# Seven products for eight inside one block product of each large product, with the sums taken in PSUM, and a re-planned order of work

## The chip, the cores and the metric

The kernel runs on one core of one Trainium2 chip. The metric is the device time of one execution in microseconds (us). The core's TensorE (PE) multiplies matrices into PSUM, VectorE (DVE) and ScalarE (ACT) read PSUM and work on tiles in SBUF, GpSimd (POOL) works on SBUF alone, and SyncE (SP) is used here only to issue DMAs. Each engine runs its own instructions in the order in which they stand, and waits on semaphores for the others.

## The reference

Inputs are x, 128 graphs of 128 nodes with 512 features, one adjacency matrix, and the weights of four layers; everything is fp32. Each layer adds a graph operation to x and normalises over the features:

```
x = layernorm(x + norm_adj @ (x @ W0) + bias)                      # layer 0
x = layernorm(x + L1(x, adj, adj, b))                              # layer 1
x = layernorm(x + (rel / norm(rel)) @ (x @ Wv.T))                  # layer 2
       where rel = adj.T * ((x @ Wq.T) @ (x @ Wk.T).T)
x = layernorm(x + elu(att @ h + beta * h))                         # layer 3
       where h = x @ W3, att = softmax(leaky_relu(s1 + s2.T) * adj)
       and s1, s2 are h times the two halves of a vector a
...
L1: A = W1 @ x;  C = W2 @ x + b;  out[o, i] = max over j of relu(A[o, j] + (C - A)[o, i])
```

In layer 1 both weights are the same adjacency, so C - A is the bias b alone, and out is the same for all features i of a row; the normalisation over the features takes such a constant away. So the kernel makes nothing for this layer but its normalisation, which it folds into that of layer 0. Layer 2's two weights Wq and Wk are folded into one matrix gq before the first group. So each group of graphs needs four large products with a 512x512 weight: w (layer 0), z and v (layer 2) and k (layer 3).

## The kernel before

Work goes in 32 groups (NG) of GB = 4 graphs, so the left side of a large product is 512x512 as well (4 graphs of 128 rows by 512 features). The seven products of `Product` split both sides into 2x2 blocks of 256x256 and make seven block products for eight, with sums and differences of blocks taken beforehand:

- `w_sum` (line 371) makes four differences of weight blocks once; they lie in a tile of four blocks, called `w_t`, `gq_t` or `wvT_t`.
- `Left.sum` makes four sums of left blocks for every group, on POOL (`pool_tt`, line 422), each 128x512; the tile is `S_y`, `S_x` or `S_n`. w has its own left side y; z and v share the sums of the transposed x; k has those of n, a later x transposed.
- `Product.make(i)` (line 540) makes block product i by four matmuls of 128x256 (two row halves, two chunks of the contraction) into one PSUM bank. `ONTO` lets products 6, 3 and 4 accumulate onto the banks of 1, 5 and 7. The order is 1, 2, 5, 7, 6, 3, 4.
- `first`, `add`, `take`, `last` carry the banks into the result: ACT copies (line 416), DVE additions of a bank and a block (line 419), and one POOL addition. For w the result is added straight into x by `d_onto` and `u_onto`.

Around the four products a group has: the aggregation with the adjacency (py, line 702), three normalisations (bn_stats and bn_aggr on DVE, a power of -0.5 on POOL in `inv_sqrt`, line 425, and the application on ACT, line 762), `pe_r` for rel (line 817), `left_times` for rel @ v and att @ h (line 866), the attention's softmax (`sc`, `pl`, `ej`, `ei`, `exp`, `rd`, `so`), and two transposes of x: `square` on DVE turns 32x32 blocks, and sixteen DMAs on SP (line 487) move them into place.

Nothing schedules this at run time. The order of every engine's work is written out by hand as strings of steps: `2.z6` is product 6 of z of group 2 counted from a base. In a name the prefixes c, d, t, u are first, add, take, last; cy, sy are the copy and the sums of y; xt, xd the turn and the move of x; nt, nd those of n; st, va, po, nb, ap the normalisation; bi the bias of layer 0. `HEAD` holds the setup (`s.`) and the first groups, `TURN` is one period of the loop and is repeated for each group in the middle, and `TAIL` holds the last groups:

```python
FIRST = 6
LAST = -10
...
for base, steps in (
    [(0, HEAD)] + [(g - BACK, TURN) for g in range(FIRST, end)] + [(end - BACK, TAIL)]
):
    for group, name in (t.split(".") for t in steps.split()):
        todo[group if group == "s" else base + int(group)].step(name)
```

PSUM gives six rotating banks of 128x512 fp32 to these steps, two more hold the vector for the attention scores (`wa_bc`). x has five buffers, the transposed left sides have three. In the setup, DVE forms that vector by eight multiplications with a sum (`q`, line 638), and PE spreads it over the partitions by eight transposes (`wa`, line 653); PE is warmed by `WARM` = 7 transposes. In the last group, k is made plainly (`k_plain`, line 792): four matmuls of 128x512 for each graph, then the copy, att @ h, elu, normalisation and the output, graph by graph.

Of the kernel before, what the change touches and what calls it, by code (L numbers as in the profile page):

```python
# [45 lines left out]
WARM = 7  # L46
GB = 4
# [15 lines left out]
1.w5 1.dw2 1.sy2 1.w7 1.dw5 0.pow 1.sy3 1.w6 1.dw7 0.nbw 2.sy2 0.apw0 1.w3 0.apw1 0.xt0 1.bi10
0.apw2 0.xt1 1.w4 0.apw3 1.dw3 2.sy3 0.xt2 1.tw 1.bi00 0.xt3 2.w1 1.dw4 0.xd 1.bi11 2.w2 2.dw1
1.bi01 2.w5 2.dw2 1.uw10 1.uw01 2.w7 2.dw5 1.uw11 1.stw0 2.w6 2.dw7 2.bi10 1.stw1 2.w3 2.tw
1.stw2 2.bi00 1.stw3 2.bi11 2.w4 2.dw3 1.vaw 2.bi01 3.y10 2.dw4 1.pow 3.y00 3.cy10 0.sx0 3.y11
3.cy00 3.y01 3.cy11 1.nbw 0.sx1 1.apw0 0.z1 1.apw1 1.xt0 0.sx2 1.apw2 1.xt1 0.z2 2.uw01 0.cz1
1.xt2 1.apw3 0.sx3 2.stw0 0.z5 3.cy01 0.dz2 2.uw10 1.xt3 0.z7 0.cz5 2.stw1 1.xd 2.uw11 0.z6
0.dz7 3.sy0 2.stw2 3.sy1 2.stw3 0.z3 0.tz 2.vaw 0.uz11 0.z4 0.dz3 2.pow 3.sy2 0.r0 0.dz4 0.r1
2.nbw 3.sy3 2.apw0 0.r2 2.apw1 3.bi10 0.r3 2.apw2 0.v1 0.rm 2.apw3 3.bi00 0.rt 0.sq0 0.sq1  # L70
3.bi11 0.wr 0.v2 0.cv1 0.sq2 3.bi01 2.xt0 0.sq3 0.v5 0.dv2 1.sx0 2.xt1 0.cr 2.xt2 0.v7 0.cv5
1.sx1 2.xt3 1.sx2 0.v6 0.dv7 0.rp 0.v3 0.tv 1.sx3 0.uv11 0.v4 0.dv3 1.z1 2.xd 0.dv4 1.z2 1.cz1
1.z5 1.dz2 1.z7 1.cz5 1.z6 1.dz7 1.z3 1.tz 1.uz11 1.z4 1.dz3 0.f0 1.dz4 2.sx0 0.f1 0.fa0 0.f2
0.stv0 2.sx1 0.f3 0.fa1 0.fa2 2.sx2 1.r0 0.fa3 1.r1 2.sx3 0.stv1 1.r2 0.stv2 1.r3 0.stv3 2.z1
1.rm 0.vav 1.sq0 1.rt 0.pov 1.sq1 2.z2 1.wr 2.cz1 0.nbv 1.sq2 0.apv0 2.z5 2.dz2 0.apv1 0.nt0
0.apv2 0.sc00 1.cr 2.z7 2.cz5 0.nt1 0.apv3 0.nt2 2.z6 1.sq3 2.dz7 1.rp 0.nt3 0.sc01 2.z3 2.tz
0.sc10 2.uz11 0.sc11 2.z4 2.dz3 0.sc20 2.r0 2.dz4 0.sc21 2.r1 0.sc30 2.r2 0.sc31 2.r3 0.pw 1.v1
2.rm 2.rt 2.sq0 2.sq1 2.wr 1.v2 1.cv1 2.sq2 2.sq3 1.v5 2.rp 1.dv2 0.pe 1.v7 1.cv5 1.v6 1.dv7
0.pl0 0.pl1 1.v3 1.tv 0.pl2 1.uv11 0.pl3 1.v4 1.dv3 0.ej 0.ei 1.f0 1.dv4 0.ex0 1.f1 0.ex1 1.fa0
0.ex2 1.f2 1.fa1 0.ex3 1.f3 1.stv0 3.w1 2.cr 0.rd 1.fa2 0.so0 0.so1 0.so2 3.w2 3.dw1 0.so3 1.fa3  # L80
3.w5 3.dw2 0.at 3.w7 1.stv1 0.aw 3.dw5 1.stv2 3.w6 3.dw7 1.stv3 0.cat 3.w3 3.tw 1.vav 3.uw01
3.w4 3.uw10 3.dw3 3.stw0 3.uw11 4.y10 0.nd 3.dw4 4.y00 3.stw1 4.cy10 1.pov 3.stw2 4.y11 4.cy00
4.bi10 3.stw3 4.y01 4.cy11 4.sy1 3.vaw 4.w1 4.cy01 1.nbv 4.sy0 1.apv0 4.w2 4.dw1 1.apv1 1.sc00
3.pow 1.apv2 1.sc01 4.w5 4.sy2 1.apv3 3.nbw 1.sc10 4.sy3 3.apw0 4.w7 4.dw5 3.apw1 4.bi00 1.sc11
3.apw2 4.w6 4.dw7 3.apw3 4.bi01 1.sc20 4.w3 4.tw 1.sc21 4.bi11 3.xt0 0.sn0 1.sc30 4.w4 3.xt1
0.sn1 3.xt2 2.v1 3.xt3 0.sn2 1.sc31 2.v2 4.dw2 2.cv1 1.pw 4.uw01 4.dw4 0.sn3 4.dw3 2.v5 2.dv2
4.uw10 4.stw0 2.v7 2.cv5 4.stw1 1.pe 4.uw11 2.v6 2.dv7 4.stw2 4.stw3 2.v3 2.tv 1.pl0 2.uv11
4.vaw 1.pl1 1.pl2 2.v4 2.dv3 1.pl3 4.pow 1.ej 2.f0 3.xd 2.dv4 2.f1 1.ei 2.fa0 2.f2 1.ex0 1.ex1
2.fa1 2.f3 1.ex2 2.fa2 0.k1 1.ex3 2.fa3 1.rd 2.stv0 0.k2 0.ck1 1.so0 1.so1 1.so2 1.so3 0.k5
0.dk2 1.at 2.stv1 0.k7 0.ck5 2.stv2 1.aw 2.stv3 0.k6 0.dk7 2.vav 4.nbw 0.k3 2.pov 0.tk 4.apw0  # L90
1.nt0 0.uk11 4.apw1 1.nt1 0.k4 0.dk3 4.apw2 3.sx0 1.nt2 4.apw3 0.h0 0.dk4 3.sx1 1.nt3 0.h1 3.sx2
0.em0 1.nd 0.h2 0.em1 0.ee0 0.h3 3.sx3 0.em2 0.ee1 3.z1 0.em3 0.ee2 0.ea0 0.ee3 0.ea1 3.z2 3.cz1
0.ea2 0.ea3 3.z5 3.dz2 0.stk0 0.stk1 3.z7 3.cz5 0.stk2 0.stk3 3.z6 3.dz7 1.cat 0.vak 2.nbv 3.z3
3.tz 0.pok 2.apv0 3.uz11 2.apv1 3.z4 3.dz3 2.apv2 1.sn0 2.apv3 3.r0 3.dz4 1.sn1 3.r1 0.nbk 2.nt0
1.sn2 3.r2 0.apk0 2.sc00 0.apk1 3.r3 0.fin0 1.sn3 2.nt1 0.apk2 0.fin1 1.k1 3.rm 0.apk3 0.fin2
2.nt2 3.sq0 0.fin3 1.k2 3.rt 1.ck1 2.nt3 3.sq1 3.wr 3.sq2 2.sc01 2.nd 1.k5 3.sq3 1.dk2 3.rp
2.sc10 1.k7 1.ck5 2.sc11 2.sc20 2.sc21 1.k6 1.dk7 2.sc30 1.k3 1.tk 2.sc31 1.uk11 1.k4 1.dk3 1.h0
1.dk4 1.h1 1.em0 5.ld 3.cr 1.h2 1.ee0 1.em1 1.ea0 1.h3 1.ee1 1.em2 3.v1 1.em3 1.ee2 2.sn0 2.pw
1.ea1 1.ee3 3.v2 1.ea2 2.sn1 3.cv1 1.ea3 2.sn2 1.stk0 3.v5 3.dv2 2.sn3 2.pe 1.stk1 3.v7 3.cv5
1.stk2 1.stk3 3.v6 3.dv7 2.pl0 1.vak 4.xt0 2.pl1 1.pok 3.v3 2.pl2 4.xt1 3.tv 1.nbk 2.pl3 4.xt2  # L100
3.uv11 1.apk0 3.v4 3.dv3 1.apk1 1.fin0 4.xt3 1.apk2 1.fin1 2.ej 5.y10 1.apk3 4.xd 3.dv4 5.y00
5.bi10 5.cy10 2.ei 5.y11 5.cy00 5.bi00 2.ex0 5.y01 5.cy11 5.sy1 3.f0 5.cy01 2.ex1 3.f1 3.fa0
5.sy0 2.ex2 3.f2 3.stv0 2.ex3 5.bi11 3.f3 3.fa1 3.fa2 5.w1 5.sy2 3.fa3 3.stv1 5.bi01 5.w2 5.dw1
5.sy3 3.stv2 1.fin2 5.w5 3.stv3 1.fin3 2.rd 3.vav 2.so0 5.w7 5.dw5 3.pov 2.so1 3.nbv 5.w6 2.so2
3.apv0 6.ld 5.dw7 4.sx0 3.apv1 3.nt0 4.sx1 3.apv2 5.w3 3.nt1 3.apv3 3.nt2 4.sx2 5.tw 3.nt3 5.w4
2.so3 5.dw2 4.sx3 2.k1 2.at 5.uw01 5.dw4 2.aw 3.sc00 2.k2 2.ck1 5.uw10 5.dw3 3.sc01 5.uw11 2.k5
5.stw0 2.cat 5.stw1 2.k7 2.ck5 5.stw2 5.stw3 2.k6 2.dk7 5.vaw 2.dk2 5.pow 3.sc10 2.k3 2.tk 5.nbw
3.sc11 2.uk11 5.apw0 2.k4 3.sc20 5.apw1 2.dk3 5.apw2 3.sc21 5.apw3 6.y10 3.nd 2.dk4 6.y00 6.cy10
6.bi10 3.sc30 6.y11 6.cy00 3.sc31 6.bi00 6.y01 6.cy11 6.sy0 4.z1 6.cy01 6.sy1 4.z2 4.cz1 6.sy2
4.z5 4.dz2 6.bi11 6.sy3 4.z7 4.cz5 6.bi01 3.pw 4.z6 4.dz7 4.z3 4.tz 5.xt0 3.sn0 5.xt1 3.pe 4.z4  # L110
# [179 lines left out]
def kernel(  # L290
# [124 lines left out]
    def copy(o, i):  # L415
        nc.scalar.copy(o, i)  # L416
# [648 lines left out]
```

## Time and profile before

| what | value |
|---|---|
| median of 3 executions | 2039.51 us (2039.47 to 2041.18) |
| the profiled execution, whole | 2038.5 us |
| its span, first to last instruction | 2036.7 us |
| PE busy | 2019.5 us, 9789 records |
| DVE busy | 1551.9 us, 3061 records |
| POOL busy | 1016.4 us, 843 records |
| ACT busy | 768.1 us, 1606 records |
| granted TensorE clock, mean | 0.998 |

The profiled execution is 1.8 us longer than its span and 1.0 us below the median. An engine's busy time is the time in which it has an instruction at work; what lies between is a wait. A fp32 matmul of the program shows as two records in the trace, each with its own weight load (PEld), so that the 28 matmuls of one large product are 56 records. A matmul's duration in a list (379 ns for 128x256) contains the overlap with its neighbours; the chain of waits, which lists work end to end, gives the time that each one takes up.

### The profile page before, as it was taken

The page shows a single profiled execution, that of the slowest core. Times are in us where ns is not written, and L with a number is a line of the kernel's source. Part 1 is how long each engine was busy: PE and PEld are TensorE (multiplying, and loading weights), DVE is VectorE, ACT ScalarE, POOL GpSimd, SP SyncE. Part 2 cuts the span into 40 slices and gives each one's busy share as a digit, 9 for nine tenths or more (in the row PEclk, how much of TensorE's full clock was granted, in tenths as well). Part 3 has the DMA queues.
Part 4 walks back from the last instruction along what each step waited for, and adds up shares of the span by engine and source line. Part 5 has one row for each costly group of instructions (what it writes and reads, how often), then busy time and mean ns, then how long its engine had stood idle before and what let it go on. Part 6 is the DMA issues. An engine that isn't in the chain of part 4 may idle for free.

```text
span 2036.7 us, 29180 instructions
## 1 busy us (share of the span) xinstructions
PE 2019.5 (99%) x9789; PEld 1700.1 (83%) x9789; DVE 1551.9 (76%) x3061; ACT 768.1 (38%) x1606; POOL 1016.4 (50%) x843
## 2 busy tenths in 40 slices
PE   8999999999999999999999999999999999999997
PEld 7888888888888888888888888888888888888884
DVE  8658765787777877777777778777777787777787
ACT  2323443433343433334333434333343333433344
POOL 6925472545445545355453455443554536544341
PEclk9999999999999999999999999999999999999999
DMA  7324543534444444444344444444444343443353
GB/s 244 53 42 68 104 99 88 104 58 93 97 91 99 78 82 93 91 93 104 63 91 97 92 100 78 80 92 93 94 92 75 88 98 85 99 92 54 67 115 88
DMA packets 736629, 184.02 MB, mean 90 GB/s; under 512 B 688864, under 2 KB 688992, under 8 KB 736480
## 3 DMA queue, kind: packets, MB, share of 16 engines
q1 hardware_dynamic: 736480, 182.16, 42.3%
q8 instruction: 78, 1.28, 0.3%
q14 instruction: 71, 0.58, 0.1%
HBM read 64.03 MB, written 49.87 MB: 56 GB/s over the span
## 4 chain that ended last, share of the span: by engine, by line
PE 98%; DVE 1%; issue 0%; ACT 0%; DMA 0%; POOL 0%; DVEq 0%; POOLq 0%
PE p_w L540 19%; PE p_v L540 19%; PE p_z L540 19%; PE p_k L540 18%; PE py L702 6%; PE pr L817 6%; PE pl_k L866 5%; PE pl_v L866 5%; PE pk L792 1%; DVE wprod L638 0%; DVE prod L885 0%; PE p_g L540 0%; DVE w_t L371 0%; DVE C_k L419 0%; DMA adj_sb<-in_adj_dram 0%
## 5 line engine op out<-in xcount | busy, mean ns | idle before, releaser
L425 POOL TENSOR_TENSOR r<-v,minus_half 128x4 f32<-128x4 f32 (+1 forms) x99 | 100.0, 1010 | 507.8 <-DVE v L748 478.4
L762 ACT ACTIVATE x<-x,nb,r 128x512 f32<-128x512 f32 x384 | 283.9, 804 | 92.6 <-DVE nb L756 80.4
L422 POOL TENSOR_TENSOR x<-x,t_w 128x512 f32<-128x512 f32 x96 | 120.8, 1287 | 161.5 <-ACT t_w L416 157.6
L419 DVE TENSOR_TENSOR x<-p_w,x 128x512 f32<-128x512 f32 x192 | 131.7, 688 | 60.9 <-PE p_w L540 48.1
L885 DVE SCALAR_TENSOR_TENSOR prod<-x,wa_bc 128x512 f32<-128x512 f32 x256 | 172.2, 673 | 4.9 <-ACT x L762 0.9
L540 PE MATMUL p_w<-w_t,S_y 128*128 128x256 f32 x768 | 171.0, 379 | 0.0
L540 PE MATMUL p_z<-S_x,gq_t 128*128 128x256 f32 x768 | 171.0, 379 | 0.0
L540 PE MATMUL p_v<-wvT_t,S_x 128*128 128x256 f32 x768 | 171.0, 379 | 0.0
L422 POOL TENSOR_TENSOR x<-x,bias_bc 128x512 f32<-128x512 f32 x128 | 162.0, 1287 | 15.8 <-DMA x_30T<-sq_x 5.9
L540 PE MATMUL p_k<-w_t,S_n 128*128 128x256 f32 x744 | 165.7, 379 | 0.9 <-DVE C_k L419 0.9
L540 PEld LDWEIGHTS p_w<-w_t,S_y 128*128 128x128 f32 x768 | 145.8, 190 | 20.0 <-issue 0.2
L540 PEld LDWEIGHTS p_z<-S_x,gq_t 128*128 128x128 f32 x768 | 145.9, 190 | 19.8
L540 PEld LDWEIGHTS p_v<-wvT_t,S_x 128*128 128x128 f32 x768 | 145.9, 190 | 19.8
L540 PEld LDWEIGHTS p_k<-w_t,S_n 128*128 128x128 f32 x744 | 141.3, 190 | 20.4 <-DVE C_k L419 1.3
L833 ACT ACTIVATE sq<-rel 128x128 f32<-128x128 f32 x128 | 39.6, 309 | 273.9 <-DVE rel L419 271.1
L702 PEld LDWEIGHTS py<-nadjT,x 128*128 128x128 f32 x1024 | 121.8, 196 | 3.2 <-DVE nadjT L605 0.8
L702 PE MATMUL py<-nadjT,x 128*128 128x128 f32 x1024 | 122.1, 279 | 0.4 <-DVE nadjT L605 0.4
L419 DVE TENSOR_TENSOR C_z<-p_z,t_z 128x512 f32<-128x512 f32 x64 | 44.1, 690 | 95.9 <-PE p_z L540 95.9
L942 DVE SCALAR_TENSOR_TENSOR e<-e,rden,beta_i 128x128 f32<-128x128 f32 x128 | 113.5, 942 | 0.9
L975 ACT ACTIVATE pl_k<-pl_k 128x512 f32<-128x512 f32 x128 | 74.2, 582 | 105.1 <-DVE x L972 101.1
L866 PE MATMUL pl_k<-C_k,attT 128*128 128x512 f32 x248 | 111.6, 592 | 0.3 <-DVE C_k L419 0.3
L866 PE MATMUL pl_v<-C_v,relT 128*128 128x512 f32 x248 | 111.5, 592 | 0.0
(1011 smaller groups left out, 4392.2 us busy)
## 6 DMA issues: line engine op xcount, KB each, us to landing
out_dram<-x SPq DMA_DIRECT2D x128, 256.0 KB, 2.1
x<-in_x_dram SPq DMA_DIRECT2D x31, 1024.0 KB, 5.7
d_r<-ru SPq DMA_DIRECT2D x31, 256.0 KB, 2.0
relT<-d_r SPq DMA_DIRECT2D x124, 64.0 KB, 2.5
s<-d_s SPq DMA_DIRECT2D x31, 256.0 KB, 3.8
d_a<-au SPq DMA_DIRECT2D x31, 256.0 KB, 2.2
attT<-d_a SPq DMA_DIRECT2D x124, 64.0 KB, 3.9
x<-in_x_dram SPq DMA_DIRECT2D x2, 512.0 KB, 4.5
```

The costliest lines, as they stand in the source:

```text
L419: nc.vector.tensor_tensor(o, a, b, f)
L422: nc.gpsimd.tensor_tensor(o, a, b, f)
L425: nc.gpsimd.tensor_tensor(o, v, minus_half[:, : v.shape[-1]], ALU.pow)
L540: nc.tensor.matmul(ps[:, j, :], lhsT=lhsT, rhs=rhs, start=(i not in ONTO and j == 0 and kc == 0), stop=(j == 1 and kc == 1), skip_group_ch ...
L702: nc.tensor.matmul(o, lhsT=self.x_chunk(b, kc), rhs=nadjT, start=True, stop=True)
L762: nc.scalar.activation(xt, xt, AF.Identity, bias=self.nb[k][:, b : b + 1], scale=self.rstd[k][:, b : b + 1],)
L817: nc.tensor.matmul(self.pr[:, b, :], lhsT=self.whole["z"][:, fc, b // 2, bass.ts(b % 2, P)], rhs=self.xT.chunk(b, fc), start=(fc == 0), st ...
L833: nc.scalar.activation(scratch, self.rel[:, b, :], AF.Square, accum_out=self.n2[:, b : b + 1])
L866: nc.tensor.matmul(ps, lhsT=left[:, b, :], rhs=self.whole[k][:, b, :], start=True, stop=True)
L885: nc.vector.scalar_tensor_tensor(prod, self.x[:, b, :], 1.0, wide(wa_bc[k]), ALU.mult, ALU.mult, accum_out=self.s[:, k, b : b + 1],)
L942: nc.vector.scalar_tensor_tensor(self.e[:, b, :], self.e[:, b, :], self.rden[:, b : b + 1], beta_i, ALU.mult, ALU.add)
L975: nc.scalar.activation(self.pz[b], self.pz[b], AF.Exp)
```

## The change

In each of w, z, v and k, block product 2 (left block (0, 1) times weight block (1, 0)) is itself made by seven products of 128x128 quarters. Its four matmuls of 128x256 become seven of 128x128, in two parts. `make_small` first writes four small products into the four quarters of the bank. ACT copies two quarters to SBUF (`before`, step b), DVE adds within the bank by three instructions (`between`, step e), and then three more small products are accumulated by PE onto what DVE left there (step 28). The order becomes 1, 5, 7, 2, 6, 3, 2 again, 4. POOL makes four more sums of quarters for each left side (`small`, step l), and DVE four differences for each weight once (`w_small_sums`, steps m). The product that makes gq in the setup stays as it was.

```diff
+    def w_small_sums(w, m):
+        b = w_small(w, m)
+        for o, p, q in (("t1", "t3", "b11"), ("t2", "b22", "t1"), ("t3", "b22", "t3"), ("t4", "b21", "t2")):
+            nc.vector.tensor_tensor(b[o], b[p], b[q], ALU.subtract)
...
+        def small(self, i):
+
+            a = lambda b, k: self.chunk(b, 2 + k)
+            self.l = big.tile([P, 4, P], F32, tag="L", name=f"L_{self.name}", bufs=2)
+            s = [self.l[:, n] for n in range(4)]
+            pool_tt(s[0], a(1, 0), a(1, 1), ALU.add)
+            pool_tt(s[2], a(0, 0), a(1, 0), ALU.subtract)
+            pool_tt(s[1], s[0], a(0, 0), ALU.subtract)
+            pool_tt(s[3], a(0, 1), s[1], ALU.subtract)
...
+        FIRST_SMALL = ((0, 0, "a11", "b11"), (1, 1, "s2", "t2"), (0, 1, "s1", "t1"), (1, 0, "s3", "t3"))
+        THEN_SMALL = ((0, 0, "a12", "b21"), (0, 1, "s4", "b22"), (1, 0, "a22", "t4"))
+
+        def make_small(self, i, then=False):
+            if not then:
+                self.banks[i] = psum.tile([P, 2, HD], F32, tag="bank", name=f"p{i}_{self.name}")
+            A, B = self.left.smalls, W2[self.weight]
+            steps = self.THEN_SMALL if then else self.FIRST_SMALL
+            for n, (r, c, a, b) in enumerate(steps):
+                lhsT, rhs = A[a], B[b]
+                if self.turned:
+                    r, c, lhsT, rhs = c, r, rhs, lhsT
+                nc.tensor.matmul(
+                    self.banks[i][:, r, bass.ts(c, P)],
+                    lhsT=lhsT,
+                    rhs=rhs,
+                    start=(not then and n == 0),
...
+        def before(self, i):
+            self.q = mid.tile([P, 2, P], F32, tag="q", name=f"q_{self.name}")
+            copy(wide(self.q), wide(self.banks[i])[:, 0 : 2 * P])
+
+        def between(self, i):
+            p = wide(self.banks[i])
+            q = self.q[:, 0]
+            tt(q, p[:, 3 * P :], q)
+            tt(p[:, 3 * P :], p[:, 2 * P : 3 * P], self.q[:, 1])
+            rest = p[:, P:].rearrange("n (c o) -> n c o", c=3)
+            tt(rest, rest, q.unsqueeze(1).to_broadcast([P, 3, P]))
```

One of each weight's four differences is now written over the weight's own block (0, 1); for the plain k of the last group a new step `rb` restores w3. The vector for the attention scores is no longer spread by PE: it goes to DRAM and comes back by a broadcast DMA (`wd`, `wb`), and ACT copies it to PSUM (`wc`). WARM becomes 11. x of the second group is loaded before the weights.

```diff
-WARM = 7
+WARM = 11
...
-FIRST = 6
-LAST = -10
+FIRST = 10
+LAST = -5
...
-        nc.vector.tensor_tensor(t[:, i], a, b, ALU.subtract)
+        nc.vector.tensor_tensor(o, a, b, ALU.subtract)
...
-    x_first = [load(0, 2)]
+    x_first = [load(0, 2), load(1)]
...
-        def wa(self):
-
-            for k in range(2):
-                for cc in range(KC):
-                    col = self.wa_[:, k, cc : cc + 1].to_broadcast([P, P])
-                    nc.tensor.transpose(wa_bc[k][:, cc, :], col, ident)
+
+        def wd(self):
+            self.d = dram.tile([2, KC, P], F32, name="d_wa", bufs=1)
+            nc.sync.dma_start(out=self.d.rearrange("k c p -> p k c"), in_=self.wa_)
+
+        def wb(self):
+            flat = self.d.rearrange("k c p -> (k c p)").partition_broadcast(P)
+            nc.sync.dma_start(out=wide(a_bc), in_=flat)
+
+        def wc(self, k):
+            copy(wide(wa_bc[k]), a_bc[:, k, :])
...
+        def rb(self):
+
+            w = w3[:, 2:4, 0:HD]
+            for o, a in ((w_block(w3, 0, 1), w_block(w3, 1, 1)), (w[:, 0, P:], w[:, 1, P:])):
+                nc.vector.tensor_tensor(o, a, o, ALU.subtract)
```

In the last group, some steps of k and what follows are split into halves of 256 columns for the last graphs (`half`, with the table `HALVES`): the last graph's att @ h, elu, statistics, application and output each come in two instructions, some of them on two engines, and its output on two DMA queues.

All three strings are written anew. One period of the loop now starts so:

```diff
 TURN = """
-4.z1 2.so0 1.apk1 1.fin0 2.so1 2.so2 1.apk2 1.fin1 2.so3 2.dk4 4.sx2 4.z2 1.apk3 1.fin2 2.at
-4.cz1 1.fin3 2.uk11 4.z5 2.aw 4.dz2 6.ld 4.sx3 4.z7 4.cz5 2.cat 4.z6 4.dz7 4.z3 4.tz 4.uz11 4.z4
...
+4.z1 4.lx2 3.fa3 3.stv1 4.z5 4.cz1 4.sx2 3.stv2 3.stv3 4.sx3 4.z7 4.cz5 3.vav 3.pov 4.z2 4.dz7
+3.nbv 4.z6 4.bz2 3.apv0 4.ez2 3.apv1 4.z3 3.nt0 4.tz 3.sc00 3.apv2 4.uz11 3.nt1 3.apv3 4.z28
+4.dz3 4.z4 4.dz2 3.nt2 5.y10 4.dz4 3.nt3 5.y00 5.cy10 5.bi10 3.sc01 3.nd 5.y11 5.cy00 5.bi00
...
+3.so0 3.so1 3.ek2 3.k3 3.tk 3.so2 3.so3 3.uk11 3.at 3.k28 3.dk3 3.aw 3.k4 3.dk2 4.f0 3.dk4 4.f1
+4.fa0 5.sx0 3.cat 4.f2 4.stv0 5.sx1 4.f3 4.fa1 4.fa2
```

In HEAD the second group's aggregation now comes before the first large product, and the steps of gq stand between later ones. HEAD covers the groups up to the tenth (`FIRST` = 10) and TAIL the last five (`LAST` = -5).

## The prediction

> **What bounds the kernel now.** I read the busy times first, then the chain of waits stage by stage, then the groups of instructions for prices, and last the timelines of PE at both ends.
>
> ```profile
> PE 2019.5 (99%) x9789; PEld 1700.1 (83%) x9789; DVE 1551.9 (76%) x3061; ACT 768.1 (38%) x1606; POOL 1016.4 (50%) x843
> PE 98%; DVE 1%; issue 0%; ACT 0%; DMA 0%; POOL 0%; DVEq 0%; POOLq 0%
> ```
>
> PE holds 98% of the chain. A busy PE need not be a PE at its peak, so the chain in order of time has to say whether work follows on work. One period of the loop:
>
> ```profile
> 976.74 12.09 PE p_w L540 x56
> 988.83 3.57 PE py L702 x32
> 992.40 12.09 PE p_v L540 x56
> 1004.49 3.43 PE pl_k L866 x8
> 1007.92 12.09 PE p_k L540 x56
> 1020.01 12.09 PE p_z L540 x56
> 1032.10 3.43 PE pl_v L866 x8
> 1035.53 3.57 PE pr L817 x32
> 1039.10 12.09 PE p_w L540 x56
> ```
>
> The reader is to see that every start is the start before plus its length: no gap in 62.36 us, and no other engine in it. So only fewer PE cycles shorten the loop, and other engines count only where they make PE wait. Prices: a large product is 28 matmuls of 128x256 in 12.09 us, 0.4318 each; py is 16 of 128x128, each with a weight block of its own, in 3.57, 0.2231 each.
>
> All PE work in the program at these prices: 128 products 1547.5, py and pr 228.7, the two att/rel products 64 x 3.43 = 219.5, the last plain k 13.7: 2009.4 us. The span is 2036.7, so 27.3 us are at the ends. The chain up to 72.39 holds three py of 3.57 and four products of 12.09 (w of three groups, gq), 59.1 of work, so 13.3 is lost at the start. At the end 8.6 follow the last matmul, and 5.4 are gaps and transposes of the last stage. The start:
>
> ```profile
> 5.54 5.11 PE py L702 x32
> 10.64 12.09 PE p_w L540 x56
> 22.73 3.47 PE p_g L540 x16
> ...
> 39.19 0.48 PE wa_bc L653
> 39.67 8.48 PE py L702 x64
> ```
>
> 5.54 before the first product, 1.54 because the first py takes 5.11 for 3.57, 4.85 in gq and `wa_bc` (22.73 to 39.67 for 12.09 of product), and 1.33 in the next py (8.48 for 7.15). The end, in the timeline of PE:
>
> ```profile
> 2022.67 3.60 PE L792 MATMUL pk<-w,n_31T 128*128 128x512 f32 x8
> 2026.10 1.96 PE L866 MATMUL pl_k<-C_k_end,attT_end 128*128 128x512 f32 x4
> ```
>
> PE is done at 2028.06; elu, statistics, power, application and output of whole 512 columns fill the rest.
>
> **What the Trainium skill says.** "TensorE: Matmul & The Clock Gate", section LDWEIGHTS, gives columns / 1.2 ns for a weight load, 107 ns for 128 columns, whatever the moving side. That is the danger of narrower matmuls: they need as many loads for less streaming. The trace has 3.57 / 32 = 111.6 ns for a 128-wide record with a load of its own, against 215.9 for a 256-wide one: still almost half, so the price for seven small ones stands. "PSUM — Partial Sum Buffer", section The four PSUM rules: writes of VectorE leave the bits alone that decide whether PE adds or overwrites, so PE can add onto what DVE left; no row of before shows it. "SBUF — State Buffer", section Who interferes with whom: a DVE instruction with two SBUF inputs waits for a GpSimd instruction that reads SBUF, with one it does not. The trace agrees; four `so` beside a busy POOL and beside an idle one:
>
> ```profile
> 1019.20 4.19 DVE L942 SCALAR_TENSOR_TENSOR e<-e,rden,beta_i 128x128 f32<-128x128 f32 x4
> ...
> 2000.36 1.13 DVE L942 SCALAR_TENSOR_TENSOR e<-e,rden,beta_i 128x128 f32<-128x128 f32 x4
> ```
>
> The three new additions each read PSUM and at most one SBUF operand, as the 128x512 ones of L419 do that keep 0.69 us.
>
> **The change part by part.**
>
> PE. Four of 0.4318 go (1.727), seven of 0.2231 come (1.562): 0.165 us for a product. There are 32 of w, z and v and 31 of k, 127: 20.9 us, 0.66 of each period.
>
> DVE. Three additions for a product. From 0.28 for a 128x128 copy out of PSUM (L606) and 0.69 for 128x512, a line gives 0.28 + 0.28 + 0.55 = 1.1 us; bounds 0.9 (neighbours overlap by 0.09) to 1.5. A period has 4.4 more on 48.5 (1551.9 / 32): 53 of 61.7, so DVE does not become the bound by its sum.
>
> ACT. A copy of 128x256, between 0.31 (128x128, L833) and 0.59 (128x512, L416): I take 0.4, 1.6 a period on 24.
>
> Where these lie. PE makes product 2's first part, then 6 and 3 (3.45 us), then the second part. In that time: 0.2 for PE's last result to be seen (0.17 in DVE's waits for pl_k), copy 0.4, additions 1.1, 0.1 for the hand-overs: 1.8. So 1.6 us of slack, if ACT and DVE are free. Reading the new TURN with these prices, z, w and v have one 0.69 addition and small instructions before their e. k has `rd`, `so0`, `so1` before it; these cost 0.28 each since POOL has nothing to do there (its next step waits for product 6), and even at the 1.05 each of the fence above the part is just in time. Cost: nothing; without the cover up to 1 us for each product of that kind.
>
> POOL. Sixteen sums of 128x128 for a period. The Trainium skill's "GPSIMD Engine Reference", section 3.1, has 4497 ns for 2048 columns, 2.2 ns each; before's 1.25 us spacing of 512 columns leaves 0.13 fixed, so 0.41 is my estimate; bounds 0.29 (another 128x128 operation at the start, of one input) and 1.29 (no cheaper than 512). 6.6 more on 31.8 a period. The tightest place is z: its L sums stand between two pairs of S sums, and the power of the v normalisation comes after them; DVE waits for that in `nb` ahead of its e. From S starting 1.9 us before z (as at 1018.10 against 1020.01): two S 2.5, L 4c, two S 2.5, power 1.0 end at 4.1 + 4c, e at 5.4 + 4c; the second part is due at 9.53. With c = 0.41 that is 7.0.
>
> SP. xd still starts when v releases the buffer, 15.3 us before the next z, as now (1004.58 for 1019.8), with the same sixteen issues. New on SP are `wd` and `wb`, in the start, behind the sixteen issues of the first x (10.7 us by the row of L487's timeline, 0.63 each). ACT's `wc0` waits for them, and queued behind it is z's first copy b; by my count of the new order the broadcast lands near 64 and the copy is due at 65.4, so I charge nothing; each us later would stall PE once.
>
> Start. The second py fills PE while w0 lands one 1 MB load later (3.3 us at the 321 GB/s of the first 20 us: 12.5 instead of 9.3); PE needs it at 14.2. The eight transposes and the DVE multiplications leave the path to the first z, and gq's steps stand where DVE has made its differences: I count 4.85 + 1.33 as gone, but 1.5 back in w0's product 2, whose four small differences come after three additions on DVE, and 0.6 at the first z, whose transposed x lands at about 59. WARM 11 fills PE up to 4.1 us and may end the slow first py (0 to 1.5 us): nothing taken. Together -4; bounds -7.7 (all but 5.54) and +2.
>
> End. Halves take about 0.7 from the last copy and matmul and 0.3 from each of five steps after it: -2.5. DVE, 85% busy from 1980 to 2010, gets two e (2.2) and `rb` (1.5) there, not all hidden: +1.5. Together -1; bounds -4 and +3.
>
> Sum on the profiled execution: 2038.5 - 20.9 - 4 - 1 = 2012.6. The median shown is 1.0 above that execution: 2013.6, forecast 2013.5.
>
> **The rivals.**
>
> *The ends give all they can* (chance 0.18). 2039.5 - 20.9 - 7.7 - 4 = 2006.9. For it: PE's start has 7.7 us of gaps that no data dependence demands. Against it: more DVE work stands in the start than before.
>
> *The second part waits* (0.22). If an e is late in the less regular orders of HEAD and TAIL, or hand-overs are longer, each 0.165 us of wait on every product costs the whole loop gain. With half of the gain gone and nothing at the ends: 2039.5 - 10.4 = 2029. For it: DVE idles 13.9 us of a period and will idle 8.7, and its order is fixed. Against it: 1.6 us of slack.
>
> *POOL's small sums are not small* (slower, 0.10). In z of every group: from c = 1.03 us the e is late, and from c = 1.23 the stall eats the whole gain (0.66 a period and 5 us at the ends). At 1.29, 5.4 + 5.16 - 9.53 = 1.03 us in 32 groups is 33 us: 2039.5 - 25.9 + 33 = 2046.6. For it: the power on 128x4 takes 1.0 us, so small POOL instructions can be dear. Against it: one input of 128x128 took 0.29.
>
> **How the numbers follow.** The likeliest, PE bound with small gains at the ends, has 0.50 and reaches from 2008 to 2019. The range 2004 to 2027 takes in most of the first rival and half of the second and leaves about 0.2 out. A measurement here can't tell 0.2% (4 us) from no change. Faster: 0.50 + 0.18 + 0.20 = 0.88; the same 0.02; slower 0.10.
>
> **What would show it.** In the chain of waits a large product of w, z, v or k should take 11.93 instead of 12.09 us and a period 61.70, with no gap before the second part. POOL's 128x128 sums should be near 0.41, the three additions near 1.1 together. The first z should start near 59 after one w less, and some 6.5 us should follow the last matmul. Wrong it would be by gaps of PE ended by DVE before the three late small products, by 128-wide records slower than 111.6 ns, or by a start with new gaps.

## The result, and the profile after

| | before | after |
|---|---|---|
| median | 2039.81 us (2038.69 to 2041.61, 7 runs) | 2034.25 us (2032.42 to 2036.59, 7 runs) |
| ratio | 1 | 0.9971, 95% interval 0.9960 to 0.9983 |
| profiled execution | 2038.5 us | 2034.25 us |
| its span | 2036.7 us | 2032.4 us |
| granted TensorE clock, mean | 0.998 | 0.995 |

The kernel became 5.6 us faster where 26 were forecast; the interval excludes no change, but the time lies above the forecast range of 2004 to 2027. First the busy times and the chain of after, by engine:

```profile
PE 2004.9 (99%) x10573; PEld 1713.8 (84%) x10573; DVE 1642.7 (81%) x3464; ACT 807.9 (40%) x1739; POOL 1175.9 (58%) x1223
PE 93%; DVE 2%; DMA 2%; SPq 1%; ACT 1%; issue 0%; POOL 0%; DVEq 0%; ACTq 0%; POOLq 0%
```

PE held 98% of the chain before, and DMA none; now DMA, DVE and SP's queue hold 5%. To see where, take the chain in order of time (start, length, what), first one period in the middle:

```profile
1040.69 3.57 PE pr L942 x32
1044.26 5.18 PE p_w L603 x24
1049.44 0.89 PE p_w L567 x8
1050.33 3.46 PE p_w L603 x16
1053.79 0.67 PE p_w L567 x6
1054.45 1.73 PE p_w L603 x8
1056.18 5.18 PE p_v L603 x24
...
1102.39 3.57 PE pr L942 x32
1105.96 4.10 PE p_w L603 x19
```

L567 is the line of the small products, L603 that of the full ones; the counts are records, two for each matmul. Four and then three small products take 0.89 and 0.67 us, the whole product 1056.18 - 1044.26 = 11.92, the period 1105.96 - 1044.26 = 61.70 instead of 62.36. No wait stands before the 0.67. The loop does what was forecast.

The same view at the start, where z of the first group is made:

```profile
65.70 9.19 DMA d_wa<-wa
...
74.91 4.76 DMA a_bc<-d_wa
...
79.69 0.04 ACT wa_bc L425
...
80.21 0.38 ACT q_z L425
...
81.98 1.62 PE p_z L567 x6
83.61 3.41 PE p_z L603 x8
87.02 3.86 PE pr L942 x32
```

This chain passes from a DMA over ACT to PE. The write `wd` of 1024 numbers took 9.19 us, the broadcast `wb` 4.76; ACT's `wc0` waited for them, z's copy `q` stood behind `wc0`, and z's second part behind that. Then the second part took 1.62 us for 0.67, product 4 took 3.41 for 1.73. PE's timeline of after shows its larger waits at both ends, but for two that the kernel before had as well (1.36 at the very start and 0.67 at 1964.84); in brackets stand the idle time before the group and what ended it:

```profile
22.51 1.06 PE L567 MATMUL p_w<-m,L_y 128*128 128x128 f32 x4 [2.48 <-DVE m L379]
53.70 0.46 PE L567 MATMUL p_w<-w,y_1T 128*128 128x128 f32 x2 [1.16 <-DVE p_w L428]
65.09 1.97 PE L603 MATMUL p_z<-x_0T,gq 128*128 128x256 f32 x8 [1.30 <-DVE wprod L700]
72.78 1.99 PE L603 MATMUL p_z<-S_x,gq_t 128*128 128x256 f32 x8 [1.19 <-POOL S_x L431]
75.33 1.99 PE L603 MATMUL p_z<-S_x,gq 128*128 128x256 f32 x8 [0.55 <-POOL S_x L431]
81.98 0.77 PE L567 MATMUL p_z<-x_0T,gq 128*128 128x128 f32 x2 [4.66 <-DVE p_z L428]
...
1985.64 0.32 PE L933 MATMUL ps<-ident,s 128*128 128x128 f32 x1 [1.21 <-DVE prod L1010]
1992.20 3.63 PE L603 MATMUL p_k<-w,S_n 128*128 128x256 f32 x8 [2.66 <-DVE x L1104]
...
2024.46 0.70 PE L906 MATMUL pz<-C_k_end,attT_end 128*128 128x256 f32 x2 [1.21 <-ACT C_k_end L425]
```

Every wait of the start but one stands in the first use of something that the change added: `m` (the weight's small differences), the additions `e` between the two parts, the late `S_x` behind POOL's small sums, the row of scores. The one is the 1.30 before z. The view names DVE, but the last of the sixteen issues of the transposed x stands at 62.7 and POOL, too, waited for that x until 65.07, so z waited for its landing. The last three lines are the tail. The 1.21 at `ps` was there before, too. At 2.66, k of the last group but one wants a PSUM bank that h of the group before has not freed. The 1.21 at the end comes with the halves.

The sum, with the prediction's prices: all PE work is 2009.4 - 20.9 = 1988.5 us, so 2032.4 - 1988.5 = 43.9 are lost at the ends, 27.3 before. At 86.81 the first pr starts. Until then PE made four py (14.28), two w (23.86), gq (12.09) and z (11.93), 62.16 of work, so 24.65 are lost; before it was 13.3. That is 11.3 us of the 16.6. Two waits inside the loop, with what they delay, are some 1.3: from the pr of group 1 to that of group 31 it takes 1814.7 us, and 1813.4 in the best version below, which has no wait there. The tail has the rest, about 4, though its last stage became shorter: 7.2 us follow the last matmul, 8.6 before.

### The profile page after: what moved, and what is told of

It reads as the page before. It is cut to its first block, busy times and chain, and to the rows that moved or that the text cites. A ratio compares the mean times of both kernels' runs of the same rounds, so it can differ in the third digit from the quotient of the medians.

```text
span 2032.4 us, 31901 instructions
## 1 busy us (share of the span) xinstructions
PE 2004.9 (99%) x10573; PEld 1713.8 (84%) x10573; DVE 1642.7 (81%) x3464; ACT 807.9 (40%) x1739; POOL 1175.9 (58%) x1223
## 2 busy tenths in 40 slices
DMA packets 737970, 184.71 MB, mean 91 GB/s; under 512 B 689936, under 2 KB 690320, under 8 KB 737808
## 4 chain that ended last, share of the span: by engine, by line
PE 93%; DVE 2%; DMA 2%; SPq 1%; ACT 1%; issue 0%; POOL 0%; DVEq 0%; ACTq 0%; POOLq 0%
PE p_z L603 16%; PE p_v L603 15%; PE p_w L603 15%; PE p_k L603 15%; PE pr L942 5%; PE pl_v L991 5%; PE py L773 5%; PE pl_k L991 5%; PE p_z L567 2%; PE p_k L567 2%; PE p_v L567 2%; PE p_w L567 2%; SPq L512 1%; DMA s<-d_s 1%; PE pk L864 1%; DMA d_wa<-wa 0%
## 5 line engine op out<-in xcount | busy, mean ns | idle before, releaser
L431 POOL TENSOR_TENSOR C_k<-C_k,t_k 128x512 f32<-128x512 f32 x31 | 40.0, 1290 | 247.1 <-ACT t_k L425 210.0
L603 PE MATMUL p_z<-S_x,gq_t 128*128 128x256 f32 x512 | 121.2, 379 | 1.2 <-POOL S_x L431 1.2
L603 PE MATMUL p_w<-w_t,S_y 128*128 128x256 f32 x512 | 122.2, 382 | 0.0
L603 PE MATMUL p_z<-S_x,gq 128*128 128x256 f32 x512 | 121.1, 379 | 0.6 <-POOL S_x L431 0.6
L603 PE MATMUL p_k<-w,S_n 128*128 128x256 f32 x496 | 118.9, 383 | 2.7 <-DVE x L1104 2.7
L603 PE MATMUL p_v<-wvT_t,S_x 128*128 128x256 f32 x512 | 121.0, 379 | 0.0
L603 PE MATMUL p_v<-wvT,S_x 128*128 128x256 f32 x512 | 121.0, 379 | 0.0
L603 PE MATMUL p_w<-w,S_y 128*128 128x256 f32 x512 | 121.0, 379 | 0.0
L603 PE MATMUL p_k<-w_t,S_n 128*128 128x256 f32 x496 | 117.2, 379 | 0.0
L603 PEld LDWEIGHTS p_z<-S_x,gq 128*128 128x128 f32 x512 | 97.2, 190 | 14.2 <-POOL S_x L431 1.0
```

Source lines behind the costliest of these rows:

```text
L431: nc.gpsimd.tensor_tensor(o, a, b, f)
L603: nc.tensor.matmul(ps[:, j, :], lhsT=lhsT, rhs=rhs, start=(i not in ONTO and j == 0 and kc == 0), stop=(j == 1 and kc == 1), skip_group_ch ...
```

## The experiments

Theory: the scheme is worth its 20.9 us in the loop, and it was given back at both ends by single waits and by the slow TensorE after them. Rivals: the scheme costs elsewhere (DVE, POOL, DMA) what it saves on PE; or the new order lost the time and the small products have no part in it.

**The row's copies late.** ACT's order in HEAD, with the load that takes the row's buffer:

```diff
-0.z2 s.wc0 1.uw01 0.z6 0.bz2 s.wc1 0.ez2 0.sx3 4.ld 1.stw0
+0.z2 1.uw01 0.z6 0.bz2 0.ez2 0.sx3 1.stw0
...
-1.apw1 1.xt0 2.bi10 0.v7 0.cv5 1.xt1 1.apw2 0.cr
+1.apw1 s.wc0 1.xt0 2.bi10 0.v7 0.cv5 1.xt1 1.apw2 s.wc1 0.cr 4.ld
```

> Only the two copies of the broadcast row into PSUM (wc0, wc1) are moved in ACT's order, from ahead of the z product's bz2 and tz of group 0 to behind the first applications of group 1, and the load of group 4, which takes the row's buffer, behind them. Theory (the scattered write of 9.19 us and the broadcast of 4.76 us hold ACT, and through ACT the TensorE): the gap of 4.66 us before z's second part goes, and with it the slow clock after it (p_z and pr took 2.9 us longer than their counts at full speed): 2034.25 - 7.5 = 2026.8, at least 2029.5 if only the gap goes. The two writes keep their 9.2 and 4.8 us. Rival (the gap hides something that is late in any case, S_x or the copies of z): at most 1.5 us faster, 2032.8 to 2035, with a new gap before pr or before the fourth product.

Measured: 2026.46 us (2025.37 to 2030.54), ratio to before 0.9935 (0.9923 to 0.9948), 7.8 us less than after. The last wait of the start is now the one before pr, in PE's timeline:

```profile
80.66 3.39 PE L938 MATMUL pr<-x_0T,C_z 128*128 128x128 f32 x28 [0.40 <-DVE C_z L424]
```

The wait of 4.66 is gone, pr starts at 79.7 instead of 86.8, and `wd` still took 8.8 us, now with nobody waiting. (The profiled run is the slowest of the five, 2030.54; what it lost in the loop is taken up below, with the load.) The theory holds.

**The row by TensorE.** `wd`, `wb` and `wc` are replaced by the eight transposes of the kernel before:

```diff
-s.wd
...
-s.wb
...
-s.wc0
+s.wa
...
-s.wc1
```

> The row reaches PSUM as in the kernel before: eight transposes on TensorE at the place of the first copy, with no write to DRAM, no broadcast and no copies on ACT. Theory: the gap of 4.66 us and the slow clock after it (2.9) go, and TensorE pays the transposes, some 1.1 to 1.8 us: 2034.25 - 6 = 2028.3, so 1.1 to 1.8 us behind the run with late copies. Rival (z waits for something else there): 2034 or slower, since the transposes are added to TensorE and the gap stays.

Measured: 2027.86 us (2027.29 to 2029.6), ratio 0.9941 (0.9929 to 0.9954): 6.4 less than after. The median is 1.4 behind the late copies, as expected, but the two ranges overlap, and the traces show no such cost: from the start of z to that of pr it takes 14.7 us in both. The transposes (71.95 to 72.99) fall into the wait for `S_x`, which shrank from 1.20 to 0.33. So which of the two routes is cheaper once nothing waits is not shown.

**The small differences of w0 early.** DVE's order:

```diff
-s.s03 0.w7 0.dw1 0.sy3 0.dw5 s.sa0 0.dw7 s.m02 s.sk0 0.w2 s.sa1 0.w6 0.bw2 0.ew2
+s.s03 s.m02 0.w7 0.dw1 0.sy3 0.dw5 s.sa0 0.dw7 0.w2 s.sa1 0.w6 0.bw2 0.ew2 s.sk0
```

> Only the small sums of w0 (m02) are moved in DVE's order, ahead of the three additions dw1, dw5, dw7, with sk0 behind ew2. DVE stood idle for 0.8, 1.0 and 1.0 us there. Theory: the gap of 2.48 us in product 2 of w0 goes, and with it the slow clock after it (1.9 us): 2034.25 - 4 = 2030.3, at least -2.4 if only the gap goes. Rival (DVE has no room; the sums, slow beside POOL, hold dw1 and with it product 6, and wk's sums become late for the product g): no gain, 2033 to 2035, with a gap before product 6 or before p_g.

Measured: 2030.86 us (2029.4 to 2033.86), ratio 0.9957 (0.9945 to 0.997), 3.4 less than after. The wait of 2.48 is gone and one of 1.23 stands before product 6, for `dw1`; pr starts at 84.1, 2.7 sooner. The theory's size was about right, and the rival had part of the truth.

**The same order with a plain product 2.** The small sums, the copy, the additions and the small products are left out in all three strings; product 2 is four matmuls of 128x256 again:

```diff
-            if i == 2 and self.weight in W2:
+            if False:
```

> The order of after with product 2 made by four products of full width again: the sums L on POOL, the small sums of the weights, the copy q, the three small products and the additions before them are left out, everything else stands where it stood. Theory (the quarter scheme is worth its whole 20.9 us in the loop and after's order gave up the rest at both ends): 2034.25 + 20.9, less what the scheme's own sums cost at the start (gap of 2.5 and slow clock of 1.9 in w0, 1.7 of waits for S_x): 2049, within 2046 to 2054; the period is 62.36. Rival (the scheme costs as much on DVE, POOL or in DMA as it saves, and the gain of 5.6 is what is left of it): 2038 to 2042, as the kernel before.

Measured: 2041.99 us (2039.26 to 2044.35), ratio to before 1.001 (1.0004 to 1.0017). The time lies in the rival's range, but the trace has a third answer. Its period is 62.36, and from the first pr to the twentieth it is slower than after by (1226.8 - 75.5) - (1225.6 - 86.8) = 12.5 us. In that stretch stand 74 large products, and 74 times the forecast 0.165 are 12.2: the scheme costs nothing in the loop. But its first pr starts at 75.5, 11.3 us before that of after. PE's timeline, where only two waits follow the first py:

```profile
61.90 3.44 PE L584 MATMUL p_z<-x_0T,gq 128*128 128x256 f32 x8 [3.23 <-DMA x_0T<-sq_x]
76.93 3.28 PE L923 MATMUL pr<-x_0T,C_z 128*128 128x128 f32 x27 [0.78 <-DVE C_z L409]
```

So the waits that I had put down in part to the order need the scheme as well: without its second part in z, PE has nothing that waits for ACT's `q`, and `wc0`, though it waits 6.84 us here, holds PE for 0.78 at most. In their traces the late copies and the early differences start pr 7.2 and 2.7 us sooner, of these 11.3. The order alone lost at the start 75.5 - 62.7 = 12.8, about the 13.3 that the kernel before lost (62.7: the 62.16 with three plain products). So the first rival is wrong for the loop, but in this order the scheme did cost 11.3 us at the start; the late copies show that it need not. The second rival is wrong for the start and the loop, but the re-planned start gained next to nothing either. The wait of 2.66 in the tail stands in this run too, so that one is the order's.

**The tail in another order.** em0, ee0 and ea0 of group 29 before sc20 of group 31, nt before sc30, pe behind the k products, rt before v4. The first steps of the changed stretch of TAIL, old and new:

```diff
-8.sc20 8.sc21 7.cat 8.sc30 8.sc31 8.nt0 8.pe 7.k1 8.pl0 6.em0 8.pl1 8.nt1 8.pl2 8.pl3 8.nt2 6.ee0
+6.em0 6.ee0 8.sc20 8.sc21 7.cat 6.ea0 7.k1 8.nt0 8.nt1 8.nt2 8.nt3 8.nd 7.ck1 7.k5 6.em1 6.ee1
```

> Only the order of the last turns is changed: em0, ee0 and ea0 of group 29 stand ahead of the dot products sc20 and sc21 of group 31 and em1, ea1 and ea2 ahead of its ej, so that the PSUM banks of h0 to h2 are free when k5, k7 and k2 of group 30 want them; the four transposes nt of group 31 stand ahead of sc30; the transposes of pe follow the k products instead of standing ahead of them; rt of group 31 stands ahead of its v4. Theory (the tail loses to waits for banks and to the slow clock after them): gone are 2.66 of waiting and 1.9 of slow clock at k5, 1.21 at ps and 0.67 at relT, some 1.1 come back because the last transpose, landing 1.5 us earlier, is then late for the last product: 2034.25 - 4.7 = 2029.5. Rival (the chain of group 31 from its normalization over the sixteen transpose DMAs sets the end in any case): 2032.5 to 2034.5, with a wait of 3 us or more before pk.

Measured: 2037.42 us (2034.83 to 2040.45), ratio 0.9986 (0.998 to 0.9993), 3.2 more than after, outside both the theory and the rival. Part of that came before the tail; from the pr of the last group to the end of the span it took 2037.4 - 1947.2 = 90.2 us, after 2032.4 - 1944.6 = 87.8. PE's timeline:

```profile
1991.07 0.49 PE L565 MATMUL p_k<-w,n_30T 128*128 128x128 f32 x2 [0.35 <-DVE x L1102]
1994.20 0.65 PE L931 MATMUL ps<-ident,s 128*128 128x128 f32 x4 [0.25 <-DVE x L1102]
...
2004.86 6.35 PE L989 MATMUL pl_k<-C_k,attT 128*128 128x512 f32 x8 [5.89 <-issue]
```

The waits for banks shrank to 0.35 and 0.25, but I had put the copy t_k behind four exponentials on ACT, and the product h waited 5.89 us for C_k. That mends easily:

```diff
-7.ek2 6.ea3 8.ej 8.ei 7.k3 8.ex0 8.ex1 8.ex2 8.ex3 8.rd 6.stk0 8.so0 8.so1 8.so2 8.so3 7.tk
+7.tk 6.em3 6.ee3 6.ea2 8.pe 8.pl0 8.pl1 8.pl2 8.pl3 7.ek2 6.ea3 7.k3 7.uk11 8.ej 7.k28 7.dk3 8.ei
```

> The tail of e5_tail with one fault of its order mended: there the copy t_k of group 30 stood on ACT behind four exponentials of group 31, and the additions into C_k on DVE behind the rows of its attention, so that h0 of group 30 waited 5.89 us. Here t_k follows product 6 at once and the additions stand ahead of the attention's. Theory (the tail loses to waits for banks and the slow clock after them): the waits of 2.66, 1.21 and 0.67 and the 1.9 of slow clock go, some 2 us come back at the last products: 2034.25 - 4.2 = 2030. Rival (what is taken from one wait at the end comes back as another, since DVE, ACT and the DMAs of group 31 have no room there): 2033 to 2037.

Measured: 2031.31 us (2029.4 to 2033.32), ratio 0.996 (0.9946 to 0.9973), 2.9 less than after; from the pr of the last group to the end 2028.8 - 1944.6 = 84.2 us, 3.6 less than after, where 4.2 were expected. PE's timeline of the tail:

```profile
1988.42 0.49 PE L565 MATMUL p_k<-w,n_30T 128*128 128x128 f32 x2 [0.36 <-DVE x L1102]
1991.99 0.65 PE L931 MATMUL ps<-ident,s 128*128 128x128 f32 x4 [0.68 <-ACT t_k L423]
...
2005.00 1.99 PE L862 MATMUL pk<-w,n_31T 128*128 128x256 f32 x8 [0.94 <-DVE attT_end L1083]
2008.01 1.12 PE L989 MATMUL pl_k<-C_k_end,attT_end 128*128 128x512 f32 x2 [1.01 <-ACT C_k_end L423]
```

In place of the waits of 2.66, 1.21 and 0.67 stand these four, 2.99 in place of 4.54, with no slow products behind them; the 1.21 before the last product stays. Most of the tail's loss was its order.

**The load behind the broadcast.** SP's order in every turn, and likewise in HEAD:

```diff
-7.ld 5.apw0 4.ev2 5.apw1 3.pe
+5.apw0 4.ev2 5.apw1 3.pe 7.ld
```

> Only SP's order: the load of 1 MB of x stands behind the broadcast of s (pe) of its turn instead of ahead of it, in HEAD and TURN. Theory (the loop's few gaps, 0.2 and 0.6 us in the profile of after, 2.1 and 2.7 in two other runs, come from e waiting behind that load): the broadcast lands in 4 us instead of 5.4 in the median, the waits of ACT for it fall from 71 us towards 30, no gap of TensorE inside the loop, 2034.25 - 1 = 2033.2. Rival (the DMA system has its slow moments whatever the order): gaps of the same size remain, 2034.3.

Measured: 2033.58 us (2032.29 to 2033.83), ratio 0.9964 (0.9952 to 0.9977); against after it can't be told from nothing. What the traces say is clearer. The list of DMA issues (count, size of one, median us to landing), first after, then this run:

```profile
s<-d_s SPq DMA_DIRECT2D x31, 256.0 KB, 5.4
```

```profile
s<-d_s SPq DMA_DIRECT2D x31, 256.0 KB, 4.3
```

ACT waited 36.5 us for it in place of 71.3, and the two waits before k's second part are gone; one of 0.38 remains in the loop, elsewhere. In the run with late copies the loop had five such waits, 3.2 us, all at products of k. One trace could be luck, but of the nine traces with small products and the load ahead eight have such waits at k, and the three with the load behind have none; nor has the run with a plain product 2, load ahead. So the small products do let the loop feel a slow DMA, by a us or three in a run.

**Products reordered at the start.** With late copies: product 2 behind 6 and 3 and its second part last in w0 and z0, and all of POOL's S_x ahead of L_x:

```diff
-0.z7 0.lx2 0.dz7 0.sx2 0.z2 1.uw01 0.z6 0.bz2 0.ez2 0.sx3 1.stw0 1.uw10 0.z3
+0.z7 0.sx2 0.dz7 0.sx3 0.z6 0.lx2 0.z3 0.tz 1.uw01 1.stw0 0.z2 1.uw10 0.bz2
```

> The late copies of the row as in e1_wc_late, and beside them the order of products at the start: in w and z of group 0 products 6 and 3 come ahead of product 2, and its second part last; in w of group 1 the second part last; the POOL sums of z's left factor all ahead of the small ones. Theory (the quarter scheme's own sums, m on DVE, L on POOL and the additions between its parts, are late in the first products, and that is all that is wrong there): against 2026.46 of e1_wc_late gone are 2.48 + 1.9 in w0, 1.74 in z0, 1.16 in w1: 2019.2. Rival (the stalls only move on to the next wait, the landing of the transposed x of group 0): 2023 to 2026, with the wait before z0 grown by as much as w0 gained.

Measured: 2031.62 us (2031.18 to 2033.14), ratio 0.9959 (0.9946 to 0.9971): 5.2 slower than with the late copies alone, and outside both the theory and the rival. Two lines of PE's timeline and one of ACT's say why:

```profile
63.97 1.97 PE L599 MATMUL p_z<-x_0T,gq 128*128 128x256 f32 x8 [3.09 <-DVE wprod L696]
80.23 0.76 PE L563 MATMUL p_z<-x_0T,gq 128*128 128x128 f32 x2 [4.34 <-DVE p_z L424]
```

```profile
76.84 0.59 ACT L421 COPY t_z<-p_z 128x512 f32<-128x512 f32 x1 [8.52 <-POOL x L427]
```

All products share one buffer `t`. z's copy into it waited for POOL to have added the t of w of group 1, which I had moved behind the small sums, and z's `q` stood behind that copy. And the wait before z grew from 1.30 to 3.09 while z started only 1.0 us sooner.

**All of it together, first try.** The start of e8_start, the tail of e5_tail, the load of e6_ld_after_pe, and in the loop k's second part behind product 4.

> All of it: the start of e8_start, the tail of e5_tail, the load behind the broadcast of e6_ld_after_pe, and in the loop's k product the second part behind product 4 instead of ahead of it, so that it has 1.7 us more to wait for DVE. Theory (the scheme is worth its 20.9 us, and what was lost was lost to the order at both ends): 2019.2 - 4.7 - 1 = 2013.5, within 2011 to 2017, faster than both kernels. Rival (the parts share a limit): 2018 to 2022.

Measured: 2031.02 us (2030.47 to 2032.06), ratio 0.9954 (0.9941 to 0.9966). Both faults are in it, 4.34 us at z and 5.89 in the tail, so it tells nothing new of the parts.

**The start, mended.** With late copies and m02 early:

```diff
-0.pow s.q02 1.w7 0.nbw
+0.pow 0.nbw s.q02 1.w7
...
-1.w28 s.sv0 1.w4
+s.sv0 1.w4 1.w28
...
-3.cy01 s.q12
+3.cy01 1.uw01 1.uw10 1.uw11 s.q12
...
+0.z7 0.sx2 0.dz7 0.sx3 0.z6 0.lx2 0.z3 0.tz 0.z2 0.bz2 0.dz3 0.ez2 0.z4 0.uz11 0.dz4 0.z28
```

> The start alone, over e1_wc_late: m02 early as in e3_m_early; nb of group 0 ahead of the dot product q02 on DVE, so that its transposed x is issued 2.3 us earlier; in w of group 1 product 4 ahead of the second part; POOL adds t_w of group 1 while it waits for the transposed x instead of between the sums of z; in z of group 0 products 6 and 3 ahead of product 2 and the second part last, with the POOL sums S_x ahead of L_x; the sums of w3 behind z. In e8_start z still lost 4.34 us because the copy t_z needs the buffer that POOL's additions of t_w had not yet read. Theory (each wait at the start has its own cause and can be taken away): gone against 2026.46 are 3.4 (w0), 1.16 (w1), 1.30 (z0), 1.74 (S_x): 2018.9. Rival (they feed one chain, the sixteen transposes of x through SP, and only move): 2023.5 to 2027, with the wait before z0 at 2.5 us or more.

Measured: 2025.6 us (2023.29 to 2027.4), ratio 0.993 (0.9917 to 0.9942), 0.9 less than with the late copies alone, in the rival's range; the ranges of the two runs overlap, so their whole times don't tell them apart. The trace does. PE's timeline after the first py:

```profile
61.36 3.55 PE L599 MATMUL p_z<-x_0T,gq 128*128 128x256 f32 x8 [3.07 <-DMA x_0T<-sq_x]
73.19 1.99 PE L599 MATMUL p_z<-x_0T,gq_t 128*128 128x256 f32 x8 [0.38 <-DVE C_z L424]
76.70 3.50 PE L938 MATMUL pr<-x_0T,C_z 128*128 128x128 f32 x29 [0.79 <-DVE C_z L424]
```

The single waits inside the products are gone, and pr starts 3.0 us earlier than with late copies. What is left is one wait, for the transposed x. The chain of e8_start, where the same wait was the bound, shows what is ahead of it; these are its last pieces there, of sixteen such issues from 52.10 on:

```profile
60.20 0.63 SPq L508
60.87 0.63 SPq L508
61.55 2.07 DMA x_0T<-sq_x
```

SP issues the sixteen DMAs of a transposed x 0.67 us apart, and those of wv before them at the same pace. This wait lay behind the others all along, as the plain run shows (3.23 before z).

**Work put into the gap.** Thirty transposes that nothing reads, between product 3 and the second part of z in the kernel after:

```diff
+            pt = bank("pt_fill")
+            for _ in range(30):
+                nc.tensor.transpose(pt[:, 0, :], ident, ident)
...
-0.z3 1.stw1
+0.z3 s.fill 1.stw1
```

> After as it is, with thirty transposes of the identity into a bank that nothing reads, put on TensorE between product 3 of group 0's z and its second part, where TensorE stands idle for 4.66 us. They add no work that anything waits for and fill 3.4 us of the gap at the speed of a busy TensorE (0.11 us each), up to 4.8 at a slower one. Theory (a stalled TensorE is slow for some microseconds after it, and that is a cost of its own beside the gap): the gap shrinks, the wait for wc0 stays, but the second part of z, product 4 and pr take 0.67 + 1.73 + 3.57 us instead of 8.89 for the three: 2034.25 - 2.9 = 2031.4. Rival (the slower products have another cause, such as the granted clock of the whole chip or POOL's traffic): 2034 to 2036.

Measured: 2032.71 us (2030.36 to 2035.94), ratio 0.9966 (0.9954 to 0.9978); its interval overlaps that of after, so the whole time doesn't decide. The trace does, for the place itself. PE's timeline of this run:

```profile
75.56 3.44 PE L680 MATMUL pt_fill<-ident 128*128 128x128 f32 x30
80.86 0.46 PE L563 MATMUL p_z<-x_0T,gq 128*128 128x128 f32 x2 [1.87 <-DVE p_z L424]
...
81.61 1.89 PE L599 MATMUL p_z<-x_0T,gq_t 128*128 128x256 f32 x8
...
84.34 3.39 PE L943 MATMUL pr<-x_0T,C_z 128*128 128x128 f32 x28 [0.40 <-DVE C_z L424]
```

PE comes to the second part as late after product 3 as it did, 3.44 + 1.87 being even more than 4.66, yet the second part, product 4 and pr took 87.57 - 80.86 = 6.71 us, against 90.72 - 81.98 = 8.74 in after. So 2.0 of the loss there is the speed of TensorE after standing idle. The granted clock says the same (the second figure from the left is the length of the stretch, the third from the right the clock; first after, then this run):

```profile
82.00:86.80 4.80, 4.80 (x14) 4.10 (x15) 3.42 (x8) 0.00 (x0) 3.85 (x6) 0.50 0.59 218
```

```profile
80.80:84.00 3.20, 3.08 (x18) 2.71 (x18) 3.10 (x8) 0.00 (x0) 3.20 (x5) 1.00 0.78 264
```

POOL is busy in both stretches, so its traffic, which the rival named, is not the reason.

**The best version.** Start of e11_start2, tail of e10_tail2, load of e6_ld_after_pe, and in TURN

```diff
-3.k28 3.dk3 3.aw 3.k4 3.dk2 4.f0 3.dk4
+3.k4 3.dk3 3.aw 3.k28 3.dk4 4.f0 3.dk2
```

> The start of e11_start2, the tail of e10_tail2, the load behind the broadcast as in e6_ld_after_pe, and in the loop the second part of k behind product 4. Theory: 2018.9 - 4.2 - 0.7 = 2014, within 2011 to 2018, faster than both kernels. Rival: 2020 to 2026, where the best so far stands.

Measured: 2019.42 us (2019.17 to 2019.52), ratio to before 0.9899 (0.9886 to 0.9913). It is 20.5 us faster than before and 14.8 faster than after, and beats every run above. Its profile has no wait of PE from the first pr to the tail. It lies 5.4 above what I expected, mainly for the one wait before z, which I had not believed in:

```profile
61.40 3.42 PE L597 MATMUL p_z<-x_0T,gq 128*128 128x256 f32 x8 [3.01 <-DMA x_0T<-sq_x]
```

With the slow products behind it (3.42 us, 1.89 at full speed) that is 4.5 us.

## Why the prediction was wrong, step by step

- **PE, -20.9.** Right. 61.70 a period, 11.92 a product, and the period of the plain run is 62.36.
- **DVE and ACT, hidden.** Right in the loop. The additions took 0.29, 0.30 and 0.57 us (1.1 was taken), the copy 0.37 (0.4). The slack was enough but not idle: where a DMA is late, it is used up, at some 1.3 us in the profiled execution.
- **POOL, 0.41 a sum.** Right in the steady loop (0.43 to 0.46). At the start the same sums took 0.66 to 0.91, side by side with sums of two SBUF inputs on DVE.
- **Start, -4, with "I charge nothing" for `wc0`.** This is the step that failed. The prediction had the broadcast "near 64" and the copy due at 65.4. The last of DVE's eight products ended at 65.68, so the write began later than the forecast landing; it took 9.19, the broadcast 4.76, and it landed at 79.67. The prediction's own clause, "each us later would stall PE once", was the right mechanism with the wrong size: the copy had gained some slack too, so the stall was 4.66 us, and taking it away was worth 7.8. The rest is "1.5 back in w0's product 2", which was 2.48 and what followed it, 3.4 by the run that undid it, and waits that were not in the sum, for S_x (1.74) and for `e` of w of group 1 (1.16). In place of -4 the start came out at +11.3. The -4 itself did not come either: the run with a plain product 2 lost 12.8 at the start where the kernel before lost 13.3. There the transposed x, forecast at "about 59" for a wait of 0.6, let z begin at 61.9 after a wait of 3.23, with slow products behind it (3.44 us for 1.89), and the first 64 records of py took 9.59 us for 7.15; with the 5.7 before the first py these are the 12.8.
- **End, -1.** The halves gave 1.4 of the 2.5 after the last matmul. In front of that, TAIL's order let k wait for a bank, which the prediction did not look for: about +4 in place of -1, of which the mended order got 3.6 back in its trace.
- **What no step had.** A TensorE that has waited is slow afterwards. The Trainium skill, "TensorE: Matmul & The Clock Gate", Part 1, says that the array runs at half its clock after an idle window of about 3.4 us and needs about as long a busy one to recover, and that the window is free-running. The traces agree on the half: the granted clock was 0.50 after the gap of 4.66 and 1.00 where the gap was filled. The kernel before shows it, too: behind the waits of 0.41 at `wa_bc` its clock was 0.50 from 39.4 to 42.2 us. But what follows a gap does not go by its length alone. After a gap of 2.48, shorter than 3.4, two small products (four records) took 1.06 us in place of 0.61; after 3.07 and 3.23 eight full-width records took 3.55 and 3.44, after 3.09 their 1.97. The same wait of 2.66 in the tail was followed by 3.63 us for eight records in after and by 1.99 in the run with a plain product 2. A window that runs free of the kernel would scatter so, but no run here isolates it.

The rival that came nearest, the second part waiting, had the right place (the second part) and named "the less regular orders of HEAD and TAIL", but priced a wait in every product. What really happened was few waits, each large: at the start nearly all where something was used for the first time, in the tail for a PSUM bank.

## What to carry to other kernels

A change that shortens the steady loop adds operands that have to exist before the first turn; follow each of them to its first use, and price its DMA by its count of pieces, not by its bytes. On an engine that works in order, a copy that waits for a long DMA belongs behind everything that TensorE waits for, even if its own data are wanted much later. And when one wait is taken away, ask which one lay behind it: at this start five other waits hid most of what the queue of DMA issues costs, and only the runs without them showed it.

## What the runs showed of the hardware

- The write of 1024 numbers of 4 bytes into 1024 places (4 KB) took 9.19 us in after and 8.8 with late copies; the writes d_a and d_r of 256 KB from 128 partitions land in 2.0 in the median. The Trainium skill, "DMA: Bandwidth & Descriptors", Rules for kernel authors, says that a strided last dimension becomes one descriptor for each element; the traces agree: the run with the row by TensorE, which has neither this write nor the broadcast, counts 688881 DMA packets under 512 bytes where after counts 689936, 1055 fewer.
- The first sixty-four records of py took 7.70 us in one run and up to 9.98 in others with the same instructions, so the start alone can move a time by 2 us.
- A difference of 128x128 on DVE with two SBUF inputs took 1.29 us in the mean beside a busy POOL (`m` of w in the first group of after) and 0.28 to 0.29 without (`m_g`).
